# A GRU scan woven into attention on one core: row order of Y, operand tiles, a subtracting scan, staged Newton steps and heads in pairs

## The chip, the cores and the metric

The kernel runs on one core of one Trainium2 chip. The metric is the device time of one execution in microseconds. The engines are TensorE (PE: matmuls; PEld: its weight loads), VectorE (DVE), ScalarE (ACT), GpSimd (POOL) and SyncE (SP), which here only issues DMAs.

## The reference

Four residual layers over x of shape (4, 512, 512); cond has shape (4, 512).

```python
# 1: attention, 16 heads of 32, with adaptive norm
scale, shift = split(cond @ W_emb + b_emb)
xn = rms_norm(x, g_norm) * (1 + scale) + shift
q, k, v = heads(xn @ W_qkv); q, k = rms_norm(q, g_q), rms_norm(k, g_k)
o = softmax(q @ k.T / sqrt(32)) @ v
x = x + o + o @ W_out
# 2: a GRU over the 512 positions, state h of (4, 512), starting from cond
gi = x_t @ W_ih + b_ih;  gh = h @ W_hh + b_hh
r = sigmoid(i_r + h_r);  z = sigmoid(i_z + h_z)
n = tanh(i_n + r * h_n)
h = (1 - z) * n + z * h;  x_t = x_t + h
# 3 and 4: causal convolutions with 4 taps per channel, taps from cond
x = x + conv(x, cond);  x = x + conv(x, cond) + b
```

## The kernel before

**Two kinds of work.** The GRU is a chain of 512 steps that can't be taken in parallel. Attention is cut into 16 blocks of 32 positions; block i must be done before step 32 i. After a setup (weights split into two float16 halves, K and V for all positions) and a ramp that does block 0, one loop over t runs the steps, and the attention of later blocks, and the convolution of earlier ones, are filled in between as tasks.

**One step.** All 512 channels of the state lie as 128 partitions by 16 columns (4 channel groups, 4 batches). PE multiplies the state by the three gates' weights with the state as the stationary operand (L1227, `mm`), into four groups of output rows at once: gates r and z into tile X (128 x 256), gate n into tile Y (128 x 128). The state is carried as three numbers: HS in float32, A its float16 rounding, and the difference. For X 32 matmuls run, 16 with A on the low half of the weights and 16 with the difference and A on the high half; for Y 32 with 16 stationary columns. Both tiles were seeded by ScalarE beforehand with the input's part (L1121 seedX, L1124 seedY) from G, which SyncE loads from a DRAM scratch GD four steps at a time (L1092, L1093).

Each group of 32 rows of Y holds for each of 4 batches 4 slots, which the scan N later runs through: the two parts of the hidden product, the input's part of gate n, and the float16 product again. The four slots of one batch are made by four of the 16 stationary columns.

Then the vector engines follow, in this order of the program: VectorE transposes X in blocks of 32 (TX, L1241) and adds its two parts (S, L1243); ScalarE takes tanh into zt (L1244), seeds X for the next step (L1121) and makes d0 = 0.5 - 0.5 zt, that is 1 - z (L1247); VectorE transposes Y (TY, L1253) and runs the scan N (L1254), which multiplies by r and adds; ScalarE's second tanh gives the first half of D1 (L1255); VectorE gives the second half (L1256) and runs the scan twice, for A (L1264) and HS (L1265), state = d0 * state + D1. Last comes `prep` for the next step: VectorE subtracts A from HS into the operand tile BT (L1130), ScalarE copies A into BT (L1131) and halves HS into HH (L1132), and GpSimd adds HS to x for the convolution (L1269, x2b).

**The queue.** `Queue` places tasks by priorities and planned costs. `head(...)` at the start of a step issues the stages that VectorE, ScalarE and GpSimd owe, within planned budgets; `pe(PE_SLOT)` issues PE's chunks behind Y's matmuls, up to 1600 planned ns a step (2000 in the first 40). A task also takes and returns buffers: PSUM banks `m` (2) and `s` (2), score buffers `P` and so on. `flush` runs the queue to the end of a block that isn't done in time. All five engines run in the order of the program.

For each head, `sch` gives 3 chunks of 4 score matmuls (L439, ps), `smax` the row maximum (L446) and its scaled negative on GpSimd (L447), `sexp` the exponential (L455), `tpch`/`tps` the transposes (L301, ptp) and their copy (L475), and `avch` the product with V (L483, po). Before that comes Q (L369), the squares' sums R with a reciprocal root by three Newton iterations on GpSimd (`rsqrt_ops`, L257 to L276), and after it the output projection WO and the gates' input parts GI (L568).

PSUM has eight banks: X, N, Y (the rest of Y's bank takes `keep_warm`'s idle matmuls), two of m, two of s, one O.

Of the kernel before, what the change touches and what calls it, by code (L numbers as in the profile page):

```python
# [16 lines left out]
P = 128  # L17
# [5 lines left out]
PE_SLOT = 1600  # L23
SC_ = 215
SLOT0, NS0 = 2000, 40
# [10 lines left out]
COLS = {SC_: 192, 680: 256, 137: 64, 150: 128, 330: 128, 140: 256, 111: 256, 123: 256}  # L36
# [126 lines left out]
def body(ctx, tc, x, cond, W_emb, b_emb, g_norm, W_qkv, g_q, g_k, W_out, W_ih, W_hh, b_ih, b_hh, L3_b, out):  # L163
# [9 lines left out]
    NN = pg.tile([P, 16, 4], F32, name="N")  # L173
    Yb = pg.tile([P, 512], F32, name="Y")
    Y, idle = Yb[:, 0:128], Yb[:, 128:512]
# [12 lines left out]
    def rowmask(n, c):  # L188
        m = cst.tile([P, 1], F32, name=n)
        nc.vector.tensor_reduce(m, ident.rearrange("p (q s) -> p q s", q=4)[:, :, c], AX.XY, ALU.add)  # L190
        return m

    mr = mz = rowmask("mr", slice(0, 4))
    mh, mn = rowmask("mh", slice(4, 8)), rowmask("mn", slice(12, 16))

# [33 lines left out]
    BT = [cst.tile([P, 4, 8, 4], F16, name=f"BT{i}") for i in range(2)]  # L229
    for i in range(2):  # L230
        nc.gpsimd.memset(ZT[i], 1.0)
        nc.gpsimd.memset(ZT[i][:, :, :, 0:1], 0.0)
        nc.gpsimd.memset(D0[i], 0.0)
        nc.gpsimd.memset(BT[i], 0.0)
# [7 lines left out]
    def keep_warm(n, to=None):  # L242

        for _ in range(n):
            nc.tensor.matmul(idle if to is None else to, zz[:, 0:128], zz[:, 0:384], start=to is not None, stop=True, skip_group_check=True)
# [73 lines left out]
    q_ = Queue(dict(m=2, s=2, O=1, P=4, PT=4, xb=3, xhl=1, QS=3, q=1, o=1, gi=1, x1=3, L=3))  # L319

    def block_tasks(i):
# [72 lines left out]
        def rs0():  # L394
            v = at("rv", [P, 16])
            rt = at("rt", [P, 4, 32])
            nc.vector.transpose(rt.rearrange("p j r -> p (j r)"), s["pr"][:, 0:128])
            nc.vector.tensor_scalar(v.rearrange("p (j q) -> p j q", j=4), rt[:, :, 0:4], 1.0 / 32, EPS, ALU.mult, ALU.add)
            rq = at("rq", [P, 16])
            s["mx"] = at("mx", [P, 16], bufs=3)  # L400
            s["nb"] = at("nb", [P, 16], bufs=3)
            s["ls"] = at("ls", [P, 16], bufs=3)
            s["rs"] = rq, v
            if not pre_q:
                rsqrt(rq, v, 16, ear, nc.gpsimd)
                rs1()
# [8 lines left out]
        if pre_q:  # L415
            R = Task(f"R{i}")
            R.started, R.done = True, 0
            for tag in ("xb", "QS", "L"):
                q_.free[tag] -= 1
        else:  # L420
            R = add(f"R{i}", deps=[Q], acq=["m", "L"], chunks=[(330, rch)], stages=[[("DVE", 410, rs0), ("Pool", 4800, lambda: None)]], rel=["m", "q"], settle=2)
# [9 lines left out]
        def sch(j, q, u):  # L431
            def f():
                if u == 0:
                    s[("s", j, q)] = pb.tile([P, 512], F32, name="ps", tag="s", bufs=2)
                t = s[("s", j, q)]
                R_ = slice(32 * q, 32 * q + 32)
                x_, k_ = (("qh", KH), ("qh", KL), ("ql", KH))[u]
                for b in range(B):
                    nc.tensor.matmul(t[32 * b:32 * b + 32, :], s[x_][R_, j, 32 * b:32 * b + 32], k_[R_, j, b, :],  # L439
                                     start=(u == 0), stop=(u == 2), skip_group_check=True)  # L440
            return f
# [17 lines left out]
        def tpch(h, ps=False):  # L459
            def piece(j):  # L460
                def f():
                    if j == 0:
                        s[("pt", h)] = pb.tile([P, 512], F32, name="ptp", tag="s" if ps else "m", bufs=2)
                    transpose4(s[("pt", h)], s["PX"][h], (j,))
                return f
            return [(150, piece(j)) for j in range(4)]
# [21 lines left out]
        for j in range(4):  # L488
            for q in range(4):
                h = 4 * j + q  # L490
                STask[h] = add(f"S{i}.{h}", h, deps=[R], acq=["s", "P"], after=last["S"], chunks=[(SC_, sch(j, q, u)) for u in range(3)],
                               stages=[[("DVE", 600, smax(j, q)), ("Pool", 150, lambda: None)], [("ACT", 720, sexp(j, q))]],
                               rel=["s"], settle=int(first))
                last["S"] = [STask[h]]
                TPs[h] = add(f"TP{i}.{h}", h, deps=[STask[h]], after=last["TP"], acq=["m", "PT"], chunks=tpch(h),
                             stages=[[("ACT", 490, tps(h))]], rel=["m", "P"], settle=int(first))
                last["TP"] = [TPs[h]]
                dep = [TPs[h]] + ([prev_av] if prev_av else [])
                AVs[h] = add(f"AV{i}.{h}", h, deps=dep, chunks=[(137, avch(h, kt)) for kt in range(4)],
                             acq=["O"] if h == 0 else [], rel=["PT"])  # L500
                prev_av = AVs[h]
# [100 lines left out]
        def tail(nx, ahead):  # L602
# [42 lines left out]
            def gik(k):  # L645
                for n in "rzn":
                    if k == 0:
                        pg[n] = pm("pgn") if n == "n" else pb.tile([P, 512], F32, name="pgi" + n, tag="s", bufs=2)
                    for m, (xa, wi) in enumerate(((xh, 0), (xl, 0), (xh, 1))):
                        nc.tensor.matmul(pg[n], xa[:, k, :], WR[n][:, wi, k, :], start=(k == 0 and m == 0), stop=(k == 3 and m == 2))  # L650
# [46 lines left out]
    with ExitStack() as pre_ctx:  # L697
# [83 lines left out]
        def x_t(i, tag=None):  # L781
            PY[i] = pb.tile([P, 512], F32, name="py", tag=tag, bufs=2 if tag == "s" else 1) if tag else pm("py")
            transpose4(PY[i], YS[i])
# [137 lines left out]
        def proj(v, kt, b):  # L921
            p = pb.tile([P, 512], F32, name="pkv", tag="s", bufs=2)
            XH, XL = XHL[kt]
            n = 0
            for k in range(4):
                for (xa, wi) in ((XH, 0), (XL, 0), (XH, 1)):
                    nc.tensor.matmul(p, xa[:, k, b, :], WKV[:, wi, k, v, :], start=(n == 0), stop=(n == 11))
                    n += 1
            return p
# [130 lines left out]
    def scan_constants():  # L1060
# [4 lines left out]
        for v, m in ((sel, 1), (selY, 2)):  # L1065
            nc.gpsimd.memset(v, 0.0)
            nc.gpsimd.tensor_scalar(v[:, :, 4 * m:4 * m + 4], ident.rearrange("p (b t) -> p t b", b=4)[:, 0:2, :], 1.0, 1.0,
                                    ALU.mult, ALU.mult)

    sel, selY = lt("sel", [P, 2, 8]), lt("selY", [P, 2, 12])  # L1070
# [3 lines left out]
    with tc.manual_schedule(engines={ENG.PE, ENG.DVE, ENG.Activation, ENG.Pool, ENG.SP}):  # L1074
        ahead = [t for t in need[1] if t.name in ("S1.0", "S1.1", "S1.2")]
# [3 lines left out]
        q_.flush(need[0] + ahead, 1700, lambda used: keep_warm(max(0, int((1050 - used) / 160))), {8: scan_constants})  # L1079
# [9 lines left out]
    def load_g(c):  # L1089
        g, i, t0_ = G[c % 2], c // 8, 4 * (c % 8)  # L1090
        for qq in range(4):
            nc.sync.dma_start(g[32 * qq + 4:32 * qq + 8, :, 0:2, :], GD[i][qq, :, t0_:t0_ + 4, 0:2, :])  # L1092
            nc.sync.dma_start(g[32 * qq + 8:32 * qq + 12, :, 2, :], GD[i][qq, :, t0_:t0_ + 4, 2, :])  # L1093
# [3 lines left out]

    def dup(v):
        return v.rearrange("p (k b) -> p k b", k=4).unsqueeze(2).to_broadcast([P, 4, 2, 4])


    def seed_first(t, y):
# [12 lines left out]
        for qq in range(4 * y):  # L1115
            r = 32 * qq
            nc.tensor.matmul(Y[r:r + 12, :], selY[:, t], gs0["n"][:, qq, :], start=False, stop=True,
# [8 lines left out]
    def prep(A, HS, t):  # L1126

        Bt = BT[t % 2]
        HH = wk.tile([P, 16], F32, name="HH", tag="HH")
        nc.vector.tensor_tensor(Bt[:, :, 0:4:2, :], dup(HS[:, :, 1]), dup(A[:, :, 1]), ALU.subtract)  # L1130
        nc.scalar.activation(Bt[:, :, 1:8:2, :], A[:, :, 1].rearrange("p (k b) -> p k b", k=4).unsqueeze(2).to_broadcast([P, 4, 4, 4]), AF.Copy)  # L1131
        nc.scalar.activation(HH, HS[:, :, 1], AF.Copy, scale=0.5)  # L1132
        return Bt, HH

# [65 lines left out]
    with tc.manual_schedule(engines={ENG.PE, ENG.DVE, ENG.Activation, ENG.Pool, ENG.SP}):  # L1200
        seed_first(0, 0)
        Bt, HH = prep(A, HS, 0)
        due = None
        for t in range(T):
# [27 lines left out]
            for k in range(4):  # L1232
                mm(X, Bt[:, k, 0:2, :].rearrange("p s b -> p (s b)"), 8, Whi, k, slice(0, 2))
            if t == 0:
                seed_first(0, 1)
            for k in range(4):
                mm(Y, Bt[:, k, 4:8].rearrange("p s b -> p (s b)"), 16, Wlo, k, slice(2, 3))
            for k in range(4):
                mm(Y, Bt[:, k, 0:4].rearrange("p s b -> p (s b)"), 16, Whi, k, slice(2, 3))
# [13 lines left out]
            nc.vector.transpose(TY.rearrange("p h j b k -> p j h k b"), Y.rearrange("p (j h k b) -> p j h k b", j=4, h=2, k=4))  # L1253
            nc.vector.tensor_tensor_scan(f(NN), f(zt[:, 0]), TY[:, 0].rearrange("p j b k -> p (j b k)"), 0.0, ALU.mult, ALU.add)  # L1254
            nc.scalar.activation(D1[:, :, 0], NN[:, :, 3], AF.Tanh, scale=0.5 * IWS)  # L1255
            nc.vector.scalar_tensor_tensor(D1[:, :, 1], zt[:, 1, :, 2], 1.0, HH, ALU.add, ALU.mult)  # L1256
# [6 lines left out]
            keep_warm(-(-(WARM - q_.cols) // 384), pm("warm")[:, 0:384] if q_.free["m"] else None)  # L1263
            nc.vector.tensor_tensor_scan(f(An), f(d0), f(D1), 0.0, ALU.mult, ALU.add)  # L1264
            nc.vector.tensor_tensor_scan(f(HSn), f(d0), f(D1), 0.0, ALU.mult, ALU.add)  # L1265
            A, HS = An, HSn
            if t + 1 < T:
                Bt, HH = prep(A, HS, t + 1)
# [30 lines left out]
```

## Time and profile before

| | |
|---|---|
| Timed runs | 1883.12, 1876.41, 1889.18 us; median 1883.12 us |
| Profiled execution | 1878.9 us, span 1876.8 us, 114,013 instructions |
| PE busy | 1655.3 us (88%) |
| DVE busy | 1344.8 us (72%) |
| ACT busy | 1220.1 us (65%) |
| POOL busy | 468.6 us (25%) |
| Mean granted clock of PE | 0.982 |

The scan's N runs 512 times, from 242.9 to 1856.7 us; what lies before is setup and ramp, what lies behind is the last convolution. Busy shares are means over all of this. A matmul's end is modelled, and matmuls overlap, so a busy PE need not be the bound; which wait ends last in a step decides that. A group's line on the page gives the program line, the engine, output and inputs, sizes, count, busy time, the mean of one in ns, and the idle time before it with what ended it.

### The profile page before, as it was taken

How to read it: one execution, taken by the hardware profiler on the slowest of the kernel's cores; microseconds unless marked ns; L12 is line 12 of the kernel's file. 1: busy time of each engine (PE TensorE's matmuls, PEld its weight loads, DVE VectorE, ACT ScalarE, POOL GpSimd, SP SyncE). 2: the span in 40 equal slices, each digit the busy share in tenths (PEclk: the TensorE clock that was granted, in tenths of full speed). 3: DMA queues.
4: the chain of work that ended last, by engine and by line, in shares of the span. 5: the costliest groups of instructions: out<-in, count | busy, mean ns of one | idle time of the engine just before them, and what ended most of it. 6: DMA issues, size and time to landing. Idle time of an engine off the chain costs nothing.

```text
span 1876.8 us, 114013 instructions
## 1 busy us (share of the span) xinstructions
PE 1655.3 (88%) x48969; PEld 1173.1 (63%) x48969; DVE 1344.8 (72%) x4948; ACT 1220.1 (65%) x4685; POOL 468.6 (25%) x1496
## 2 busy tenths in 40 slices
PE   5788889999999999999999999999999998987553
PEld 2443557667676767676767666676667676765442
DVE  4784467786778777877777777878777877776664
ACT  4542466776767776767676767676676767665543
POOL 1366001222213131222222131313131222121112
PEclk9998899999999999999999999999999999999998
DMA  5652020101010102010101010010101010101000
GB/s 184 226 191 91 25 68 18 50 18 34 18 35 13 39 16 60 13 39 13 40 12 34 19 49 25 19 35 13 39 13 40 13 34 12 35 13 34 11 17 10
DMA packets 68921, 78.11 MB, mean 42 GB/s; under 512 B 6560, under 2 KB 54720, under 8 KB 67776
## 3 DMA queue, kind: packets, MB, share of 16 engines
q1 hardware_dynamic: 68416, 70.82, 12.5%
q8 instruction: 385, 6.31, 1.4%
q14 instruction: 120, 0.98, 0.2%
HBM read 44.58 MB, written 26.21 MB: 38 GB/s over the span
## 4 chain that ended last, share of the span: by engine, by line
PE 47%; DVE 24%; ACT 10%; DMA 8%; issue 6%; SPq 3%; POOL 2%; DVEq 0%; ACTq 0%; POOLq 0%
PE X L1227 21%; PE ps L439 6%; DVE TX L1241 5%; PE Y L1227 5%; PE pgi L568 5%; DMA G<-GD 5%; DVE TY L1253 4%; PE ptp L301 4%; DVE N L1254 4%; ACT D L1255 3%; DVE A L1264 2%; PE po L483 2%; ACT X L1121 2%; SPq L1093 2%; ACT Y L1124 1%
## 5 line engine op out<-in xcount | busy, mean ns | idle before, releaser
L1227 PEld LDWEIGHTS <-BT 128*8 128x8 f16 (+1 forms) x24576 | 450.2, 88 | 82.5 <-issue 19.1
L1227 PE MATMUL X<-Wlo,A 128*4 128x256 f16 x8192 | 313.1, 272 | 126.4 <-DVE A L1264 88.9
L1269 POOL TENSOR_TENSOR x2b<-x,HS 128x16 f32<-128x16 f32 x512 | 126.8, 248 | 1130.7 <-DVE HS L1265 1129.4
L1244 ACT ACTIVATE ZT<-S 128x32 f32<-128x32 f32 x512 | 134.9, 264 | 415.8 <-DVE S L1243 415.3
L1241 DVE STREAM_TRANSPOSE TX<-X 128x256 f32<-128x256 f32 x512 | 229.2, 448 | 210.0 <-PE X L1227 208.9
L1227 PE MATMUL X<-Whi,BT 128*8 128x256 f16 x8192 | 316.0, 273 | 2.7 <-issue 2.4
L1227 PEld LDWEIGHTS <-A 128*4 128x4 f16 x8192 | 151.4, 82 | 219.1 <-DVE A L1264 192.4
L1253 DVE STREAM_TRANSPOSE TY<-Y 128x128 f32<-128x128 f32 x512 | 205.2, 401 | 11.1 <-PE Y L1227 5.0
L1227 PE MATMUL Y<-Whi,BT 128*16 128x128 f16 x8192 | 209.2, 219 | 4.3 <-issue 4.0
L1227 PE MATMUL Y<-Wlo,BT 128*16 128x128 f16 x8192 | 207.9, 219 | 4.2 <-issue 3.7
L1121 ACT ACTIVATE X<-G 128x256 f32<-128x256 f32 x510 | 202.4, 397 | 1.1 <-DMA G<-GD 0.9
L455 ACT ACTIVATE PX<-ps,nb,rqs 128x512 f32<-128x512 f32 x256 | 195.1, 762 | 8.7 <-POOL nb L447 4.8
L1254 DVE TENSOR_TENSOR_SCAN N<-ZT,TY 128x64 f32<-128x64 f32 x512 | 153.3, 299 | 54.9 <-ACT ZT L1244 1.9
L446 DVE TENSOR_REDUCE mx<-ps 128x1 f32<-128x512 f32 x256 | 174.8, 683 | 16.0 <-PE ps L439 15.9
L1264 DVE TENSOR_TENSOR_SCAN A<-D,D 128x32 f16<-128x32 f32 x512 | 115.2, 225 | 94.2 <-ACT D L1255 91.5
L301 PE MATMUL ptp<-ident,PX 128*128 128x128 f32 x1024 | 173.3, 290 | 1.0 <-ACT gs L576 0.6
L1131 ACT ACTIVATE BT<-A 128x64 f16<-128x64 f16 x512 | 131.2, 256 | 52.8 <-DVE A L1264 4.6
L301 PEld LDWEIGHTS ptp<-ident,PX 128*128 128x128 f32 x1024 | 111.4, 143 | 81.7 <-issue 43.1
L475 ACT ACTIVATE PT<-ptp 128x512 f32<-128x512 f32 x248 | 143.3, 582 | 15.7 <-PE ptp L301 15.7
L1124 ACT ACTIVATE Y<-G 128x128 f32<-128x128 f32 x510 | 141.6, 278 | 1.0 <-DMA G<-GD 0.5
L483 PEld LDWEIGHTS po<-V,PT 128*32 128x32 f32 x8192 | 99.1, 112 | 62.5 <-issue 53.8
L483 PE MATMUL po<-V,PT 128*32 128x32 f32 x8192 | 131.1, 200 | 7.3 <-issue 6.5
(266 smaller groups left out, 2818.7 us busy)
## 6 DMA issues: line engine op xcount, KB each, us to landing
GD<-gs SPq DMA_DIRECT2D x45, 256.0 KB
G<-GD SPq DMA_DIRECT2D x512, 16.0 KB
G<-GD SPq DMA_DIRECT2D x512, 8.0 KB
xp<-in_x_dram SPq DMA_DIRECT2D x16, 256.0 KB
xb<-in_x_dram SPq DMA_DIRECT2D x16, 256.0 KB
xhl<-XD SPq DMA_DIRECT2D x32, 128.0 KB
out_dram<-ob SPq DMA_DIRECT2D x16, 256.0 KB
wst<-in_L_cond_W_qkv_dram SPq DMA_DIRECT2D x6, 512.0 KB
```

Of the source, the lines that this page charges most:

```text
L301: nc.tensor.transpose(dst[:, 128 * j:128 * j + 128], src[:, 128 * j:128 * j + 128], ident)
L446: nc.vector.tensor_reduce(s["mx"][:, h:h + 1], s[("s", j, q)], AX.X, ALU.max)
L455: nc.scalar.activation(pe_, s[("s", j, q)], AF.Exp, bias=s["nb"][:, h:h + 1], scale=s["rqs"][:, h:h + 1], accum_out=s["ls"][:, h:h + 1])
L475: nc.scalar.activation(pt_, s[("pt", h)], AF.Copy)
L483: nc.tensor.matmul(s["po"][32 * b:32 * b + 32, 32 * h:32 * h + 32], s["PT"][h][:, kt, 32 * b:32 * b + 32], V[:, 4 * b + kt, 32 * h:32 * h ...
L1121: nc.scalar.activation(X.rearrange("p (g c) -> p g c", g=2), G[(t // 4) % 2][:, t % 4, 0:2, :], AF.Copy)
L1124: nc.scalar.activation(Y, G[(t // 4) % 2][:, t % 4, 2, :], AF.Copy)
L1227: nc.tensor.matmul(dst[32 * qq:32 * qq + M, :], lhs, W[:, k, cols].rearrange("p g (j q s) -> p q g j s", j=4, q=4)[:, qq], start=False, st ...
L1241: nc.vector.transpose(TX.rearrange("p a r -> p (a r)"), X)
L1253: nc.vector.transpose(TY.rearrange("p h j b k -> p j h k b"), Y.rearrange("p (j h k b) -> p j h k b", j=4, h=2, k=4))
L1254: nc.vector.tensor_tensor_scan(f(NN), f(zt[:, 0]), TY[:, 0].rearrange("p j b k -> p (j b k)"), 0.0, ALU.mult, ALU.add)
L1264: nc.vector.tensor_tensor_scan(f(An), f(d0), f(D1), 0.0, ALU.mult, ALU.add)
```

## The change

- **Rows of Y.** The 16 stationary columns go by batch and then slot, where they went by slot and then batch. TY's output is then contiguous in runs of 16. Slots are ordered A, difference, difference, A, and both weight halves use the same columns. The seeds' rows in G, the masks for the biases and selY move with them.
- **Operand tiles.** BX for X (two slots) and BY for Y (four) take the place of BT. VectorE subtracts for BX, GpSimd for BY; ScalarE copies A into both.
- **The state's scan subtracts.** D1's first half is tanh of the negative argument, its second (d0 - 1) * HS, and the two scans compute d0 * state - D1. HH goes.
- **Newton steps.** R's reciprocal root is issued in three further stages, one iteration each, in place of one.
- **Heads in pairs.** A task SP issues the score matmuls of two heads by turns, with a planned cost of 225 for 8 matmuls. N moves into columns 128 to 191 of Y's bank, and s gets a third bank. `keep_warm` writes only to a free m bank.
- **Budgets.** PE_SLOT 1550 for 1600, the first 40 steps 1900 for 2000.

```diff
-PE_SLOT = 1600
-SC_ = 215
-SLOT0, NS0 = 2000, 40
+PE_SLOT = 1550
+SC_ = 225
+SLOT0, NS0 = 1900, 40
...
-    NN = pg.tile([P, 16, 4], F32, name="N")
-    Y, idle = Yb[:, 0:128], Yb[:, 128:512]
+    Y, NN = Yb[:, 0:128], Yb[:, 128:192].rearrange("p (a k) -> p a k", k=4)
...
-q_ = Queue(dict(m=2, s=2, ...
+q_ = Queue(dict(m=2, s=3, ...
...
             if not pre_q:
-                rsqrt(rq, v, 16, ear, nc.gpsimd)
-                rs1()
+                s["nw"] = rsqrt_ops(rq, v, 16, ear, nc.gpsimd)
+                next(s["nw"])
+                next(s["nw"])
+
+        def rsp(last):
+            def f():
+                for _ in range(3 if not last else 9):
+                    next(s["nw"], None)
+                if last:
+                    rs1()
+            return f
...
-  stages=[[("DVE", 410, rs0), ("Pool", 4800, lambda: None)]], rel=["m", "q"], settle=2)
+  stages=[[("DVE", 410, rs0)]] + [[("Pool", 700, rsp(n == 2))] for n in range(3)], rel=["m", "q"], settle=1)
...
                 for b in range(B):
-                    nc.tensor.matmul(t[32 * b:32 * b + 32, :], s[x_][R_, j, ...], k_[R_, j, b, :], ...)
+                    for r in (q, q + 1):
+                        R_ = slice(32 * r, 32 * r + 32)
+                        nc.tensor.matmul(s[("s", j, r)][32 * b:32 * b + 32, :], s[x_][R_, j, ...], k_[R_, j, b, :], ...)
...
+                if q % 2 == 0:
+                    SP = add(f"SP{i}.{h}", h, deps=[R], acq=["s", "s", "P", "P"], after=last["S"],
+                             chunks=[(SC_, sch(j, q, u)) for u in range(3)], settle=1)
...
-            nc.sync.dma_start(g[32 * qq + 8:32 * qq + 12, :, 2, :], GD[i][qq, :, t0_:t0_ + 4, 2, :])
+            nc.sync.dma_start(g[32 * qq + 2:32 * qq + 18:4, :, 2, :], GD[i][qq, :, t0_:t0_ + 4, 2, :])
...
     def prep(A, HS, t):
-        Bt = BT[t % 2]
-        HH = wk.tile([P, 16], F32, name="HH", tag="HH")
-        nc.vector.tensor_tensor(Bt[:, :, 0:4:2, :], dup(HS[:, :, 1]), dup(A[:, :, 1]), ALU.subtract)
-        nc.scalar.activation(Bt[:, :, 1:8:2, :], A[:, :, 1]...to_broadcast([P, 4, 4, 4]), AF.Copy)
-        nc.scalar.activation(HH, HS[:, :, 1], AF.Copy, scale=0.5)
-        return Bt, HH
+        Bx, By = BX[t % 2], BY[t % 2].rearrange("p k b s -> p (k b) s")
+        h4, a4 = (v[:, :, 1].rearrange("p (k b) -> p k b", k=4) for v in (HS, A))
+        two = lambda v: v[:, :, 1].unsqueeze(2).to_broadcast([P, 16, 2])
+        nc.vector.tensor_tensor(Bx[:, :, 0], h4, a4, ALU.subtract)
+        nc.gpsimd.tensor_tensor(By[:, :, 1:3], two(HS), two(A), ALU.subtract)
+        nc.scalar.activation(Bx[:, :, 1], a4, AF.Copy)
+        nc.scalar.activation(By[:, :, 0:4:3], two(A), AF.Copy)
+        return Bx, BY[t % 2]
...
-            nc.vector.transpose(TY.rearrange("p h j b k -> p j h k b"), Y.rearrange("p (j h k b) -> p j h k b", j=4, h=2, k=4))
+            nc.vector.transpose(TY.rearrange("p h j b k -> p j h (b k)"), Y.rearrange("p (j h r) -> p j h r", j=4, h=2))
             nc.vector.tensor_tensor_scan(f(NN), f(zt[:, 0]), TY[:, 0]..., 0.0, ALU.mult, ALU.add)
-            nc.scalar.activation(D1[:, :, 0], NN[:, :, 3], AF.Tanh, scale=0.5 * IWS)
-            nc.vector.scalar_tensor_tensor(D1[:, :, 1], zt[:, 1, :, 2], 1.0, HH, ALU.add, ALU.mult)
+            nc.scalar.activation(D1[:, :, 0], NN[:, :, 3], AF.Tanh, scale=-0.5 * IWS)
+            nc.vector.scalar_tensor_tensor(D1[:, :, 1], d0[:, :, 1], 1.0, HS[:, :, 1], ALU.subtract, ALU.mult)
...
-            keep_warm(-(-(WARM - q_.cols) // 384), pm("warm")[:, 0:384] if q_.free["m"] else None)
-            nc.vector.tensor_tensor_scan(f(An), f(d0), f(D1), 0.0, ALU.mult, ALU.add)
-            nc.vector.tensor_tensor_scan(f(HSn), f(d0), f(D1), 0.0, ALU.mult, ALU.add)
+            if q_.free["m"]:
+                keep_warm(-(-(WARM - q_.cols) // 384), pm("warm")[:, 0:384])
+            nc.vector.tensor_tensor_scan(f(An), f(d0), f(D1), 0.0, ALU.mult, ALU.subtract)
+            nc.vector.tensor_tensor_scan(f(HSn), f(d0), f(D1), 0.0, ALU.mult, ALU.subtract)
```

## The prediction

> **What bounds the kernel now.** Part 4 of the profile page comes first, and it misleads here: it puts a fifth of the chain on the scan's matmuls and a sixth on attention work (ps, pgi, ptp, po), as if TensorE were the bound.
>
> ```profile
> PE X L1227 21%; PE ps L439 6%; DVE TX L1241 5%; PE Y L1227 5%; PE pgi L568 5%; DMA G<-GD 5%; DVE TY L1253 4%; PE ptp L301 4%; DVE N L1254 4%; ACT D L1255 3%; DVE A L1264 2%; PE po L483 2%; ACT X L1121 2%; SPq L1093 2%; ACT Y L1124 1%
> ```
>
> Ends of matmuls are modelled, so that chain crosses to TensorE wherever a filler's modelled end passes the start of X. The view of the waits is firmer: nearly every step has ScalarE waiting for S, VectorE for X, and TensorE's weight load for A.
>
> ```profile
> ACT ZT L1244 <- DVE S L1243: 415.3, 470, 2.3
> DVE TX L1241 <- PE X L1227: 208.9, 420, 1.8
> PEld L1227 <- DVE A L1264: 192.4, 343, 1.6
> ```
>
> So I read one plain step in the timeline, engine by engine: VectorE, ScalarE, and the weight load that opens the next step (start, length, engine, line). This step's X began at 1003.03.
>
> ```profile
> 1004.12 0.45 DVE L1241 STREAM_TRANSPOSE TX<-X 128x256 f32<-128x256 f32 x1 [0.81 <-PE X L1227]
> 1004.61 0.19 DVE L1243 TENSOR_TENSOR S<-TX 128x32 f32<-128x32 f32 x1
> 1004.72 0.40 DVE L1253 STREAM_TRANSPOSE TY<-Y 128x128 f32<-128x128 f32 x1
> 1005.22 0.30 DVE L1254 TENSOR_TENSOR_SCAN N<-ZT,TY 128x64 f32<-128x64 f32 x1
> 1005.43 0.16 DVE L1256 SCALAR_TENSOR_TENSOR D<-ZT,HH 128x16 f32<-128x16 f32 x1
> 1005.77 0.22 DVE L1264 TENSOR_TENSOR_SCAN A<-D,D 128x32 f16<-128x32 f32 x1 [0.18 <-ACT D L1255]
> 1005.91 0.20 DVE L1265 TENSOR_TENSOR_SCAN HS<-D,D 128x32 f32<-128x32 f32 x1
> ```
> ```profile
> 1004.83 0.27 ACT L1244 ACTIVATE ZT<-S 128x32 f32<-128x32 f32 x1 [1.46 <-DVE S L1243]
> 1004.97 0.40 ACT L1121 ACTIVATE X<-G 128x256 f32<-128x256 f32 x1
> 1005.31 0.21 ACT L1247 ACTIVATE D<-ZT 128x16 f32<-128x16 f32 x1
> 1005.55 0.18 ACT L1255 ACTIVATE D<-N 128x16 f32<-128x16 f32 x1
> ```
> ```profile
> 1006.09 0.32 PEld L1227 LDWEIGHTS <-A 128*4 128x4 f16 x16 [0.23 <-DVE A L1264]
> ```
>
> The step is 3.06 us, and it is a chain: X's matmuls 1.09, TX to S 0.49, S to TY 0.11, TY to N 0.50, N to the second tanh 0.33, tanh to A 0.22, A to the next X 0.32. A's line says what it waited for: 0.18 us for ScalarE's tanh. Counted over the trace, the next X starts 0.055 us after A's end in 456 of 511 steps, fillers or not. The tile view has N from 242.9 to 1856.7, a mean step of (1856.7 - 242.9)/511 = 3.16 us; the last two blocks, with little filler, go at 3.02. So 0.14 x 511 = 72 us lies above the bare chain: about 25 of it VectorE or TensorE being late with TX, 15 TY starting late, 25 X starting late after A, of which 17 in the first 64 steps (the longest one 5.6 us at step 61, the flush of block 2).
>
> **The change, part by part.**
>
> **TY in row order.** TY now writes with a 16-byte stride and takes 401 ns. The contiguous transpose of the same size, rt, takes 308; the new one writes runs of 16 floats. So its price lies between 308 and 401; I take 308.
>
> ```profile
> L1253 DVE STREAM_TRANSPOSE TY<-Y 128x128 f32<-128x128 f32 x512 | 205.2, 401 | 11.1 <-PE Y L1227 5.0 <-ACT D L1247 1.6 <-ACT ZT L1244 1.4
> ...
> L397 DVE STREAM_TRANSPOSE rt<-pr 128x128 f32<-128x128 f32 x16 | 4.9, 308 | 0.0
> ```
>
> N would start at 1005.13 for 1005.22 (it also needs ZT, done at 1005.10), and tanh and all after it 0.09 earlier. That would be 0.09 x 511 = 46 us, if tanh stayed the last thing A waits for.
>
> **The state's scan subtracts.** It doesn't stay so. L1256 now reads zt and HH, both long done, and runs in the shadow of tanh. The new line reads d0, which ScalarE makes at L1247, and that instruction stands behind the seed of X (0.40 us), where the diff leaves it. d0 ends at 1005.31 + 0.21 = 1005.52. VectorE starts 0.03 after ScalarE's end (A after tanh), so D1 starts at 1005.55 instead of 1005.43 and ends at 1005.71. A depends on D1 on its own engine and also on ScalarE; N is such a scan with two waits, and it starts 0.10 after TY's end (1005.12 to 1005.22). So A starts at 1005.81 instead of 1005.77. Behind D1 in VectorE's queue stand A and HS, behind A the next X. The wait for tanh is gone and one for D1 takes its place: **0.04 us later per step, whatever TY gains**. Worked through for every step with its own times it is 0.039 in the median and 0.046 in the mean, since in a quarter of the steps d0 lies later against A: 512 x 0.046 = +23.6 us. In some hundred steps X starts late for TensorE's sake anyway and swallows its share, about 4: **+19 us**. HH (203 ns) leaves ScalarE at the step's start, where ScalarE waits for S 415 us over the run: nothing.
>
> **Operand tiles.** ScalarE writes 16 and 32 elements instead of 64 and HH: two instructions either way (203 for 16, 264 for 32, against 256 and 203), and X's second half needs them 0.43 after X's start, when they are done by 0.2. VectorE's subtract falls from 32 to 16 elements (192 to some 175 ns, D1's row being 163); this counts only where VectorE's other work delays TX, some 90 steps: -1.4 us. GpSimd gets a new subtract of 32 elements: between x2b's 248 (16) and 456 (128), near the lower; I take 0.28. It starts with HS's end, as x2b does, 0.14 after X's start, and ends at 0.42; Y's matmuls begin 0.87 after X. The 0.45 us between are its cover; without it Y, and then TY, come later one for one. X2b queues behind it, and nobody in the step waits for that. As for the port between the two engines: BT beside x2b takes 192 ns, the same as S alone, but 0.35 at 1006.14 beside GpSimd's 0.46 us tap.
>
> The Trainium skill's "SBUF — State Buffer", section "Who interferes with whom", speaks against this part: a VectorE instruction with two SBUF inputs contends with a GpSimd instruction that reads SBUF. By the rule the new subtract could stretch VectorE's own each time; by the row of BT beside x2b it doesn't. With 0.35 for every step X's second half would start 0.1 later, +50 us; I follow the row and put nothing in the sum.
>
> **Newton in stages.** 14 GpSimd instructions of 0.22 at a spacing of 0.30 held x2b back by 2.3 us (1003 to 1005.32). Split, a step gets 4 (1.2 us) or 6 (1.8 us), so the new subtract is not behind them. Cost on the path nothing; the scores of a block may start two steps later, and one m bank is held three steps more. Steady blocks finish their last gate at step 310 when 318 is due, so there is room.
>
> **Heads in pairs, N in Y's bank.** N moves so that scores have three banks; all users of that bank are ordered already (Y, TY, N, tanh, seed of Y), so no wait. A block has 48 chunks at 0.216; in pairs 24 of about 0.23. That two heads do run side by side is in the trace, where the last chunk of one head meets the first of the next:
>
> ```profile
> 199.32 0.40 PE L439 MATMUL ps<-KH,ql 32*32 32x512 f16 x4
> 199.33 0.39 PE L439 MATMUL ps<-KH,qh 32*32 32x512 f16 x4
> 199.56 0.38 PE L439 MATMUL ps<-KL,qh 32*32 32x512 f16 x4
> ```
>
> The second starts 0.01 after the first, not 0.22, and both together take 0.24. So 10.4 - 5.5 = 4.9 us of TensorE per block, 73 over 15. It is hidden: the fillers end before A does. What counts is the first 64 steps with their 17 us of late X: budgets 1900 for 2000 and fewer chunks, -3.4; the flush of 5.6 us misses its date by one step and I give it even odds of going, -2.5 (0 to -5.6). The ramp before the scan (176 to 221 us) waits for VectorE and ScalarE by turns: -1.5 (-4 to +3). The changed masks, the seeds' rows 4 apart and keep_warm's condition keep their counts of instructions and of DMAs (512 of 8 KB), which land steps ahead: 0.
>
> **Sum:** 19.3 - 3.4 - 2.5 - 1.4 - 1.5 = +10.5 us on the profiled execution's 1878.9 (span 1876.8 and 2.1 around it): 1889.4. The three timed runs have a median of 1883.1, 4 above that execution, so I say **1890**. Its own range: the chain from 15 (more swallowed) to 24, the rest from -14 to 0, and a few us for another order of the queue: 1876 to 1910.
>
> **Rivals.**
>
> **D1's wait costs nothing.** If tanh stays last, A comes 0.09 earlier: 46 us, of which a quarter of the steps lose some part, because fillers issue to within 0.2 us of X: -35, with the small terms -9: 1835. For it: A idles for tanh 503 times. Against: d0's place behind the seed is plain in the timeline.
>
> **TensorE is the bound after all**, as part 4 says. Then half of ps's 6% (53 us) goes: 1878.9 - 53 + 19 = 1845. Against: the constant 0.055.
>
> **The GpSimd subtract sets the pace (slower).** If VectorE's subtract is stretched to 0.35 beside it, X's second half comes 0.1 later in each step: 1890 + 51 = 1941. It decides from 0.1 us of stretch on, since the operand is ready about 0.1 before its matmul. The BT row speaks against it.
>
> **Pairs run one after the other (slower).** Then a chunk takes 0.43 for 0.225 planned; three make 0.62, of which 0.3 is idle time: 120 x 0.3 = 36: 1926. Against: the 0.01 us above.
>
> **Chances.** Forecast 0.80, free wait 0.09, TensorE 0.04, GpSimd 0.04, pairs 0.03. 1% is about what a measurement of this kernel can tell from no change, 19 us. Faster by more: 0.09 + 0.04 = 0.13. Slower by more: 0.07 and the forecast's upper part, 0.14, together 0.21. Within: 0.66. The range goes down to 1845 to take in the TensorE case and up to 1912; left out are 0.09 below and 0.07 above and a little of the tails.
>
> **What would show it.** Right: D1 starts about 0.12 later after X than now and 0.03 after d0's end; A no longer waits for tanh but 0.10 after D1; bare steps of the last blocks at 3.06 instead of 3.02; TY near 310 ns; ps chunks of 8 matmuls 0.23 apart; TensorE's busy share down by 3 to 4 points. Wrong: bare steps at 2.93, A still on tanh, or TX later than 1.10 after X.

## The result, and the profile after

The changed kernel takes 1914.24 us, the median of four runs (1907.47 to 1915.57); the kernel before, four runs on the same chip, 1883.55 us (1876.41 to 1889.18). The ratio is **1.0164**, 95% interval 1.0135 to 1.0192: slower by 1.6%. The forecast was 1890 with a range up to 1912. The profiled execution after took 1907.47 us (span 1905.7) against 1878.9 (span 1876.8): +28.6.

Part 4 of the page after, the chain that ended last, by engines and by lines:

```profile
DVE 34%; PE 31%; ACT 20%; issue 7%; DMA 3%; POOL 2%; DVEq 1%; SPq 1%; ACTq 0%; POOLq 0%
PE X L1238 22%; DVE TX L1252 10%; ACT X L1130 7%; DVE A L1276 6%; ACT ZT L1255 5%; DVE S L1254 4%; DVE D L1267 4%; ACT D L1258 3%; PE ps L450 2%; DVE mx L457 2%; DVE x L1172 2%; PE Y L1238 2%; ACT PX L466 1%; PE ptp L301 1%; DVEq L1276 1%
```

It has moved from TensorE to VectorE: TX has 10% for 5%, A 6% for 2%, and D1 (L1267), which had no place, 4%. The page's first part has PE's busy time down from 88% to 82% of the span, more than the 3 to 4 points that were forecast.

```profile
PE 1571.8 (82%) x48986; PEld 1150.6 (60%) x48986; DVE 1332.9 (70%) x4948; ACT 1247.8 (65%) x4685; POOL 563.1 (30%) x2006
```

So 83 us of TensorE's work are gone and the kernel is longer. The view of the waits after (what waited, on what; us in total, times, longest):

```profile
PEld L1238 <- DVE A L1276: 312.7, 403, 3.5
PE X L1238 <- DVE A L1276: 228.0, 372, 3.3
...
DVE A L1276 <- ACT D L1266: 12.9, 46, 0.4
```

In the kernel before, the last of these lines was:

```profile
DVE A L1264 <- ACT D L1255: 91.5, 503, 0.7
```

TensorE's weight load waits for A for 313 us where it waited 192, and A waits for the second tanh in 46 steps where it did in 503. The timeline of a step without attention work (step 490; X began at 1818.08) shows what A waits for instead, on VectorE and on ScalarE, and then the next step's weight load:

```profile
1819.18 0.45 DVE L1252 STREAM_TRANSPOSE TX<-X 128x256 f32<-128x256 f32 x1 [0.24 <-PE X L1238]
1819.66 0.19 DVE L1254 TENSOR_TENSOR S<-TX 128x32 f32<-128x32 f32 x1
1819.77 0.31 DVE L1264 STREAM_TRANSPOSE TY<-Y 128x128 f32<-128x128 f32 x1
1820.18 0.30 DVE L1265 TENSOR_TENSOR_SCAN Y<-ZT,TY 128x64 f32<-128x64 f32 x1
1820.59 0.18 DVE L1267 SCALAR_TENSOR_TENSOR D<-D,HS 128x16 f32<-128x16 f32 x1
1820.90 0.22 DVE L1276 TENSOR_TENSOR_SCAN A<-D,D 128x32 f16<-128x32 f32 x1
```
```profile
1820.02 0.39 ACT L1130 ACTIVATE X<-G 128x256 f32<-128x256 f32 x1
1820.35 0.21 ACT L1258 ACTIVATE D<-ZT 128x16 f32<-128x16 f32 x1
1820.57 0.19 ACT L1266 ACTIVATE D<-Y 128x16 f32<-128x16 f32 x1
```
```profile
1821.17 0.32 PEld L1238 LDWEIGHTS <-A 128*4 128x4 f16 x16 [1.58 <-DVE A L1276]
```

Three places are to be read here. D1 (L1267) starts at 1820.59, 0.03 after d0 (L1258) ended at 1820.56: as forecast. D1 takes 0.18 and A starts at 1820.90, **0.13 after D1's end** and not 0.10. And tanh (L1266) starts 0.09 after N's end (1820.48), where it was 0.03 before; that one is hidden here, since tanh ends 0.14 before A starts. The step lasts 3.10 us; the kernel before has 3.02 there.

Two more views: the groups of TY, and the score matmuls in PE's timeline after.

```profile
L1264 DVE STREAM_TRANSPOSE TY<-Y 128x128 f32<-128x128 f32 x512 | 158.1, 309 | 8.6 <-PE Y L1238 4.2
```
```profile
999.74 0.41 PE L450 MATMUL ps<-KH,qh 32*32 32x512 f16 x8
999.96 0.40 PE L450 MATMUL ps<-KL,qh 32*32 32x512 f16 x8
1000.18 0.40 PE L450 MATMUL ps<-KH,ql 32*32 32x512 f16 x8
```

TY takes 309 ns instead of 401, and a chunk of eight matmuls comes every 0.22 us: both parts do what was forecast of them.

### The profile page after: what moved, and what is told of

Same layout as the page of the kernel before. It is cut to its first block, busy times and chain, and to the rows that moved or that the text cites. A ratio compares the mean times of both kernels' runs of the same rounds, so it can differ in the third digit from the quotient of the medians.

```text
span 1905.7 us, 115633 instructions
## 1 busy us (share of the span) xinstructions
PE 1571.8 (82%) x48986; PEld 1150.6 (60%) x48986; DVE 1332.9 (70%) x4948; ACT 1247.8 (65%) x4685; POOL 563.1 (30%) x2006
## 4 chain that ended last, share of the span: by engine, by line
DVE 34%; PE 31%; ACT 20%; issue 7%; DMA 3%; POOL 2%; DVEq 1%; SPq 1%; ACTq 0%; POOLq 0%
PE X L1238 22%; DVE TX L1252 10%; ACT X L1130 7%; DVE A L1276 6%; ACT ZT L1255 5%; DVE S L1254 4%; DVE D L1267 4%; ACT D L1258 3%; PE ps L450 2%; DVE mx L457 2%; DVE x L1172 2%; PE Y L1238 2%; ACT PX L466 1%; PE ptp L301 1%; DVEq L1276 1%
## 5 line engine op out<-in xcount | busy, mean ns | idle before, releaser
L1141 POOL TENSOR_TENSOR BY<-HS,A 128x32 f16<-128x32 f32 x512 | 127.3, 249 | 1135.3 <-DVE HS L1277 1114.2
L1238 PE MATMUL X<-Whi,BX 128*8 128x256 f16 x8192 | 316.8, 273 | 1.9 <-issue 1.2
L1238 PEld LDWEIGHTS <-BY 128*16 128x16 f16 x16384 | 276.4, 90 | 25.2 <-issue 11.8
L1238 PE MATMUL Y<-Whi,BY 128*16 128x128 f16 x8192 | 208.6, 219 | 5.1 <-issue 5.0
L1238 PEld LDWEIGHTS <-BX 128*8 128x8 f16 x8192 | 178.0, 86 | 53.0 <-issue 4.8
L1238 PE MATMUL Y<-Wlo,BY 128*16 128x128 f16 x8192 | 207.5, 219 | 3.0 <-issue 1.5
L1265 DVE TENSOR_TENSOR_SCAN Y<-ZT,TY 128x64 f32<-128x64 f32 x512 | 153.5, 300 | 56.4 <-ACT X L1130 2.3
L301 PE MATMUL ptp<-ident,PX 128*128 128x128 f32 x1024 | 164.2, 286 | 4.6 <-ACT PX L466 1.4
L1264 DVE STREAM_TRANSPOSE TY<-Y 128x128 f32<-128x128 f32 x512 | 158.1, 309 | 8.6 <-PE Y L1238 4.2
L1142 ACT ACTIVATE BX<-A 128x16 f16<-128x16 f16 x512 | 110.9, 217 | 47.3 <-DVE A L1276 2.5
```

The source lines that it names most:

```text
L301: nc.tensor.transpose(dst[:, 128 * j:128 * j + 128], src[:, 128 * j:128 * j + 128], ident)
L1238: nc.tensor.matmul(dst[32 * qq:32 * qq + M, :], lhs, W[:, k, cols].rearrange("p g (j q s) -> p q g j s", j=4, q=4)[:, qq], start=False, st ...
L1264: nc.vector.transpose(TY.rearrange("p h j b k -> p j h (b k)"), Y.rearrange("p (j h r) -> p j h r", j=4, h=2))
```

## The experiments

Below, the **floor** is the step that 10% of the 511 steps stay under, measured from X's first matmul to the next X's: the bare chain. What the steps take beyond 511 floors is called the **rest** (mostly attention's delays), and the **ramp** is the time up to the first X. All three are read from one profiled execution of each kernel; starts and lengths given in ns or to 0.001 us are medians over the steps. The diffs are shortened, and parts of them are put in words. Before: floor 3.018 us, rest 72 us, ramp 240.2 us. After: 3.100, 66 and 233.0. So the chain gave 511 x 0.082 = 42 us, and rest and ramp gave 13 back.

**Theory 1:** the loss lies in the chain from N to A, in the number of engines that tanh and A wait for and in D1's dependence on d0. **Theory 2:** it lies on the side of attention and of the operand tiles.

Two pieces are first put alone into the kernel before.

**e3, the subtracting scan alone**

```diff
-D1[..., 0] = tanh(0.5 * N);   D1[..., 1] = (zt + 1) * HH
+D1[..., 0] = tanh(-0.5 * N);  D1[..., 1] = (d0 - 1) * HS
-scan(A, HS): d0 * state + D1
+scan(A, HS): d0 * state - D1
```

> The kernel before with only the subtracting scan (D1 from d0 and HS, no HH). Theory 1: D1 starts at d0's end, 2.515 us after X's start, takes 0.176, and A follows 0.10 later, at 2.79 instead of 2.74: 0.05 x 511 = 26 us more than before, about 1909 us. Theory 2: no change, 1883 us.

Measured: 1905.78 us, ratio 1.0128 [1.0092, 1.0165]; floor 3.076. This one edit costs 58 ns a step, more than the 39 that the prediction gave it. D1 starts 0.03 after d0 as forecast, but takes 176 ns with d0 and HS as operands, 163 with zt and HH. A starts 0.103 after D1's end, as the prediction took from N. So 13 of the missing 19 ns are D1's length. Step 490 shows it, VectorE first and then ScalarE:

```profile
1818.78 0.18 DVE L1254 SCALAR_TENSOR_TENSOR D<-D,HS 128x16 f32<-128x16 f32 x1
1819.06 0.23 DVE L1262 TENSOR_TENSOR_SCAN A<-D,D 128x32 f16<-128x32 f32 x1
```
```profile
1818.54 0.21 ACT L1245 ACTIVATE D<-ZT 128x16 f32<-128x16 f32 x1
1818.79 0.18 ACT L1253 ACTIVATE D<-N 128x16 f32<-128x16 f32 x1
```

**e4, pairs, N in Y's bank, the third score bank and the budgets alone**

```diff
-NN = pg.tile([P, 16, 4], F32, name="N")
+NN = Yb[:, 128:192]
-Queue(dict(m=2, s=2, ...
+Queue(dict(m=2, s=3, ...
+SP: score matmuls of two heads by turns; SC_ 225, PE_SLOT 1550, SLOT0 1900
```

> The kernel before with only the attention side of the change: heads in pairs, N in Y's bank, a third score bank, the new budgets; Newton, operand tiles, row order and D1 as before. Theory 1: tanh reads N from a tile that TensorE also writes and gets a second wait, so it starts 0.06 later, which is now on the path: +30 us; the ramp gains 7 and the later X of the first blocks about 10: about 1896 us. If the bank costs nothing on the path, only the gains are left: about 1866 us. Theory 2 (the attention side is the loss): 1905 us or more.

Measured: 1890.24 us, ratio 1.0042 [1.0023, 1.0061]; floor 3.082, rest 58, ramp 233.7. The attention side gains: 14 us of rest (the flush at step 61 is gone) and 6.6 of ramp. The floor loses 64 ns, 33 us. The timelines of step 490, VectorE and then ScalarE, show where:

```profile
1804.11 0.30 DVE L1258 TENSOR_TENSOR_SCAN Y<-ZT,TY 128x64 f32<-128x64 f32 x1
1804.31 0.16 DVE L1260 SCALAR_TENSOR_TENSOR D<-ZT,HH 128x16 f32<-128x16 f32 x1
1804.72 0.23 DVE L1269 TENSOR_TENSOR_SCAN A<-D,D 128x32 f16<-128x32 f32 x1 [0.24 <-ACT D L1259]
```
```profile
1804.50 0.19 ACT L1259 ACTIVATE D<-Y 128x16 f32<-128x16 f32 x1
```

N ends at 1804.41 and tanh starts at 1804.50. The profile names N's tile "Y" now, and that is the point: tanh reads a tile that TensorE writes, so it waits for TensorE's semaphore as well as VectorE's, though Y's matmuls are long done when N ends. The trace's record of semaphores bears this out: in the kernel before, tanh itself waits for VectorE, and in e4 a separate semaphore instruction of 17 ns ahead of it does, while tanh itself waits for TensorE. The second wait costs 60 ns (94 instead of 33, medians over the steps), and here it is on the chain, because tanh is the last thing A waits for.

The next two change one thing in the kernel after.

**e1, d0 ahead of the seed of X on ScalarE**

```diff
+nc.scalar.activation(d0[:, :, 1], zt[:, 1, :, 2], AF.Copy, scale=-0.5, bias=0.5)
 seedX(t + 1)
-nc.scalar.activation(d0[:, :, 1], zt[:, 1, :, 2], AF.Copy, scale=-0.5, bias=0.5)
```

> The changed kernel with one swap on ScalarE: d0 is made before the seed of X, not behind it. Theory 1 (the loss sits between N and A): D1 no longer waits for d0 and ends under tanh, at about 2.49 us after X's start instead of 2.69; A then follows tanh's end (2.68), about 0.09 behind it because A waits for three engines, so at 2.77 instead of 2.82: 0.05 x 511 = 26 us less, about 1888 us. Theory 2 (the loss is on the attention side: pairs, queue, banks): D1 moves but the time stays within 5 us of 1914.

Measured: 1908.66 us, ratio to before 1.0133 [1.0102, 1.0165]; floor 3.073. The waits show the chain change hands:

```profile
DVE A L1276 <- ACT D L1266: 142.0, 505, 3.5
```

A waits for tanh in 505 steps again, so D1's wait is gone, and still the floor is 55 ns over that of before. d0 must await zt's end, so it begins 0.29 after zt's start where the seed had begun 0.14 after it. In the last two blocks the seed then ends at 2.60 after X's start and tanh begins at 2.54, where it began at 2.50 in the kernel after, and A starts 87 ns behind tanh instead of 32. Taking D1's wait away brought the chain onto the seed ahead of tanh and onto the waits of tanh and A.

**e2, GpSimd copies the difference out of BX**

```diff
-nc.gpsimd.tensor_tensor(By[:, :, 1:3], two(HS), two(A), ALU.subtract)
+nc.gpsimd.tensor_scalar(BY[..., 1:3], Bx[:, :, 0] twice, 1.0, 1.0, ALU.mult, ALU.mult)
```

> The changed kernel, but GpSimd makes its half of BY by copying the difference from BX, so it no longer reads A. Theory 1: A's write then has no wait for GpSimd; its waits go from three to two and it follows D1's end by 0.10 us instead of 0.13: 0.028 x 511 = 14 us less, about 1900 us. If GpSimd's work or the port were what costs, a later start of this copy (it now waits for VectorE's subtract) would make it no faster or slower: 1914 or more.

Measured: 1927.81 us, ratio 1.0236 [1.0206, 1.0266]; floor 3.123. A's start falls from 0.132 to 0.103 after D1's end, now that GpSimd no longer reads A. But GpSimd now reads BX, as the view of the waits shows:

```profile
POOL BY L1141 <- DVE BX L1140: 1149.9, 490, 19.2
```

So BX's next writer, VectorE's subtract, must wait for GpSimd as well as for VectorE. Its distance from HS's end is 0.03 in the kernel after (the first two lines) and 0.10 in e2 (the last two):

```profile
1817.94 0.20 DVE L1277 TENSOR_TENSOR_SCAN HS<-D,D 128x32 f32<-128x32 f32 x1
1818.17 0.17 DVE L1140 TENSOR_TENSOR BX<-HS,A 128x16 f16<-128x16 f32 x1
```
```profile
1837.13 0.20 DVE L1277 TENSOR_TENSOR_SCAN HS<-D,D 128x32 f32<-128x32 f32 x1
1837.43 0.18 DVE L1140 TENSOR_TENSOR BX<-HS,A 128x16 f16<-128x16 f32 x1
```

The subtract starts 0.165 after X's start instead of 0.095, X's second half at 0.49 instead of 0.435, TX at 1.147 instead of 1.097. 29 ns were won at A and 50 lost at BX. The wait wasn't removed but moved to another instruction of the chain. That this edit comes out slower was not foreseen.

From here on parts of the change are undone one after another. **e5, N in SBUF; e6, D1 from zt and HH again; e7, both; e8, e7 with GpSimd taking the float16 state from BY, ScalarE's copy, instead of from A:**

```diff
 # e5, e7, e8
-NN = Yb[:, 128:192]
+NN = cst.tile([P, 16, 4], F32, name="N")
 # e6, e7, e8
+nc.scalar.activation(HH, HS[:, :, 1], AF.Copy, scale=0.5)
-D1[..., 1] = (d0 - 1) * HS;  scans subtract
+D1[..., 1] = (zt + 1) * HH;  scans add
 # e8
-nc.gpsimd.tensor_tensor(By[:, :, 1:3], two(HS), two(A), ALU.subtract)
 nc.scalar.activation(By[:, :, 0:4:3], two(A), AF.Copy)
+nc.gpsimd.tensor_tensor(By[:, :, 1:3], two(HS), By[:, :, 0:1] twice, ALU.subtract)
```

> The changed kernel with N in SBUF instead of Y's bank. Theory 1: tanh loses its wait for TensorE and ends some 40 ns earlier, but A waits for D1, which waits for d0, and comes at 2.82 us after X's start as before: no gain, 1914 us within 6. If the time were lost in Y's bank itself, the 30 us that the pairs alone seem to cost there (0.06 us a step) would come back: about 1884.

> The changed kernel with D1 from zt and HH again (scans add). Theory 1: D1 is out of the way; tanh ends at 2.68 after X's start, late by its wait for TensorE, and A follows 0.09 behind it because it still waits for three engines: 2.77 instead of 2.82, 0.05 x 511 = 27 us less, about 1887 us. If the subtracting scan were the whole loss: all of 80 ns a step, about 1873 us or less.

> As e6, with N in SBUF. Theory 1: tanh has one wait and starts 0.06 earlier, and takes some 25 ns more from SBUF; A at about 2.73 after X's start: 20 us less than e6, about 1867 us. If two waits on one instruction cost nothing: as e6.

> As e7, and GpSimd takes its float16 state from BY, where ScalarE has put it, instead of from A, so A's write needn't wait for GpSimd. Theory 1: A follows tanh by 0.03 instead of 0.09, at about 2.68 after X's start; bare steps 2.96 us against 3.02 in the kernel before: about 1839 us, faster than both kernels. The subtract on GpSimd starts some 0.25 us later and still ends before Y's matmuls at 0.87; if it doesn't, TY is late and the time is above 1870.

Measured, all four against 1873.11 us of before on their chip:

| | us | ratio, interval | floor |
|---|---|---|---|
| e5 | 1910.85 | 1.0202 [1.0172, 1.0232] | 3.102 |
| e6 | 1884.83 | 1.0058 [1.0036, 1.0080] | 3.046 |
| e7 | 1878.68 | 1.0019 [0.9997, 1.0040] | 3.025 |
| e8 | 1855.19 | 0.9896 [0.9862, 0.9931] | 2.970 |

e5 leaves the floor where it was: while D1 is last, tanh's extra wait costs nothing. e6 takes 54 ns off, and with it tanh is last again, so that e7 against e6 shows tanh's wait in its own price: 60 ns less wait, 43 more because tanh takes 229 ns from SBUF and 186 from PSUM, and N 7 less. e8 against e7 shows the third wait of A. VectorE and ScalarE in e7:

```profile
1794.44 0.23 DVE L1279 TENSOR_TENSOR_SCAN A<-D,D 128x32 f16<-128x32 f32 x1 [0.28 <-ACT D L1269]
```
```profile
1794.12 0.23 ACT L1269 ACTIVATE D<-N 128x16 f32<-128x16 f32 x1
```

and in e8:

```profile
1776.43 0.23 DVE L1279 TENSOR_TENSOR_SCAN A<-D,D 128x32 f16<-128x32 f32 x1 [0.23 <-ACT D L1269]
```
```profile
1776.17 0.23 ACT L1269 ACTIVATE D<-N 128x16 f32<-128x16 f32 x1
```

Tanh ends at 1794.35 and A starts at 1794.44; in e8, 1776.40 and 1776.43. The arithmetic is the same and so is the order of the engines. In e7 A must wait for GpSimd to have read its tile; in e8 GpSimd reads BY, and A waits for VectorE and ScalarE alone: 55 ns of floor, 23 us of time. **e8 beats both kernels**, but by less than was expected: its floor is the expected one within 0.01, while its rest is 81 us (77 in e7, 72 in the kernel before), so that part of the chain's gain was lost to attention's delays.

Last, the same edits without the pairs. **e9 is the kernel before with row order, operand tiles and Newton stages; e10 is e9 with GpSimd reading BY; e11 is e10 with pairs and their budgets, but two score banks, N keeping its own; e12 is e10 with Newton in one stage.**

```diff
 # e9, e10, e11, e12: rows of Y, BX and BY; D1 from zt and HH, scans add, N in a bank of its own
 # e10, e11, e12
-nc.gpsimd.tensor_tensor(By[:, :, 1:3], two(HS), two(A), ALU.subtract)
+nc.gpsimd.tensor_tensor(By[:, :, 1:3], two(HS), By[:, :, 0:1] twice, ALU.subtract)
 # e11
+SP for two heads, acq s, s, P, P; SC_ 225, PE_SLOT 1550, SLOT0 1900; s=2
 # e12
-stages=[[("DVE", 410, rs0)]] + [[("Pool", 700, rsp(n == 2))] for n in range(3)]
+stages=[[("DVE", 410, rs0), ("Pool", 4800, lambda: None)]]
```

> The kernel before with the order of the rows of Y by batch and slot (TY as one contiguous transpose), the operand tiles BX and BY (GpSimd's subtract reads HS and A) and the Newton steps in three stages; D1 from zt and HH with scans that add, N in a bank of its own, heads singly and the budgets as before. Theory 1 (the loss sits in the chain from N to A, in what each instruction there waits for): N comes at 2.10 us as in the changed kernel, tanh waits for one engine and runs 2.435 to 2.62, A waits for three engines (GpSimd reads A) and starts 0.087 after tanh, at 2.71 instead of 2.742; floor step 2.985 to 2.99 against 3.017, 15 to 17 us of 511 steps, so about 0.991 of the time before. Theory 2 (what was lost lies on the attention side, in the tiles or the Newton stages as much as in the chain): not faster than before, 0.998 or more.

> The kernel of the run above, but GpSimd takes the float16 state for its subtract from BY (ScalarE's copy) instead of from A, so that no GpSimd instruction reads A. Theory 1: A waits for two engines again and starts 0.032 after tanh, at 2.65; floor step 2.93; a further 25 to 28 us off, about 0.976 of the time before, less what late attention work takes back (in the kernel with N in SBUF and this edit it took some 10 us), so 0.975 to 0.982. Theory 2: no more than 0.3% from the run above.

> The kernel of the run above with the heads' score matmuls in pairs and the budgets of the changed kernel, with two score banks only, since N keeps a bank of its own. What the pairs are worth: the ramp before the scan 6 to 7 us shorter as in the run of the pairs alone, 0.003 below the run above, if two banks are enough. If a pair that needs both banks at once holds up the queue, X starts late after A by more than the 25 ns a step of before, and the time is above the run above: by 5 to 25 us.

> The kernel of the second run of this call (rows, tiles, GpSimd reads BY) with the Newton steps in one stage of 14 GpSimd instructions, as before the change. The prediction held that the stages cost nothing and serve to keep GpSimd's subtract on time: if the subtract stands behind 14 instructions of some 0.3 us in one or two steps of each of 14 blocks, the matmuls of Y wait for it by 1 to 3 us there: 20 to 40 us over the second run. If the instructions fall where the subtract is not due, or DVE's order keeps them apart: within 5 us of it.

Measured against 1877.16 us of before; rest and ramp from the profiled executions, in us:

| | us | ratio, interval | floor | rest | ramp |
|---|---|---|---|---|---|
| e8 (above) | 1855.19 | 0.9896 [0.9862, 0.9931] | 2.970 | 81 | 237.9 |
| e9 | 1896.94 | 1.0107 [1.0073, 1.0140] | 2.989 | 100 | 244.7 |
| e10 | 1880.78 | 1.0015 [0.9994, 1.0037] | 2.935 | 109 | 252.5 |
| e11 | 1943.91 | 1.0348 [1.0314, 1.0382] | 2.933 | 170 | 243.4 |
| e12 | 1879.76 | 1.0022 [0.9998, 1.0047] | 2.936 | 119 | 252.4 |

The floors are those that theory 1 gave, within 6 ns, and the times are not: it had e9 at 0.991 and e10 at 0.976. The chain's gain goes back in full to the rest and the ramp. In e9 and e10 the step at 61, where block 2 is flushed, takes 13.7 and 13.3 us (8.6 before), and steps 189 and 349 take 10.0 to 10.1 each (3.3 and 3.0 before). So theory 2 holds here: the queue without pairs doesn't finish these blocks in time. It isn't the short chain alone that does it, since e12 below has the same floor without these flushes; Newton's stages have a part in it. Set e8 beside e10: e8's floor is 35 ns longer (18 us) and yet its ratio is 0.012 lower (22 us). Pairs with a third bank, and their budgets, are then worth some 40 us (by the table 28 of rest, 19 of them in the steps 61, 189 and 349, and 15 of ramp), where on the chain of before, with Newton in one stage (e4), they were worth 21. The 15 are uncertain, because the ramp differs between executions of one kernel (last section).

e11 shows that the bank is part of it. A pair takes both banks at once, and with two of them 43 steps take over 4 us (7 before), the longest 12.2. Its time is 63 us over e10, where 5 to 25 were expected if the banks hold up the queue. The ramp, 9 us shorter than e10's in these executions, is 3 us longer than that of before.

e12 is a miss in the other direction. GpSimd's subtract does stand behind Newton there; the waits of e12 show Y late for it:

```profile
DVE TY L1261 <- PE Y L1235: 27.9, 25, 1.8
PEld L1235 <- POOL BY L1138: 27.5, 17, 2.1
```

In e10 the same two lines are:

```profile
DVE TY L1262 <- PE Y L1236: 6.1, 16, 1.2
PEld L1236 <- POOL BY L1139: 0.4, 2, 0.2
```

But the time is that of e10: in e12 the steps 61, 189 and 349 take 8.6, 3.1 and 2.9 us. One stage costs some 22 us at Y, three stages cost two flushes and a longer one in this kernel, some 19 us. The prediction's "Cost on the path nothing" holds for the stages in the kernel after as far as the flushes go, and not here. In the kernel after, with pairs, there are no such flushes at 189 and 349; what the stages are worth there wasn't tried.

## Why the prediction was wrong, step by step

**The mechanism was right.** D1 becomes last, starts 0.12 later and 0.03 behind d0, and TY's gain of 0.09 is lost: e3 has the loss without TY's gain at all, e5 shows that nothing on tanh's side counts while D1 is last.

**The step that failed is the size of the chain's term**, "0.039 in the median and 0.046 in the mean", from "A starts at 1005.81". By the trace's segments, summed over the steps, TY's start to A's start costs +46.1 us where +23.6 stood. The missing 22.5 are D1's 176 ns for 163 (13 ns, seen alone in e3) and A's start 0.132 after D1 for 0.103 (29 ns, gone in e2; e8 takes the same wait away where tanh is last). Together 42 ns x 511 = 21 us. The row taken for A's start, N behind TY, has two waits. A has three: VectorE, ScalarE, and GpSimd, which must have read A's old tile. The prediction followed what the new subtract writes forward, and found 0.45 us of cover before Y; it is 0.42 in the trace, and Y is not late. It didn't follow it backward, to the next writer of what it reads.

**"All users of that bank are ordered already (...), so no wait"** was wrong in the same way: the order made the wait useless, not absent. It costs tanh 60 ns, hidden in the kernel after, and 31 us on the path in e4.

**The small terms.** X late after A gave -10.1 where -4, -3.4 and -2.5 stood, right in the sum; but the flush at step 61 stayed (7.7 us), so the odds on it were lost and made up elsewhere, by luck as far as the runs tell. TX and what delays it: +2.9 instead of -1.4. TY after S: -2.6 for nothing. The ramp: -7.2, outside its bounds of -4 to +3. It goes with the granted clock (last section), which no step of the prediction looked at.

The sum: 46.1 + 2.9 - 2.6 - 10.1 - 7.2 = +29.1 against +28.9 of span. The forecast of the profiled execution missed by 18 us; the other 6 are the distance from that execution, the shortest of the four, to their median. The prediction had read a distance of 4 for the kernel before and did not add it.

**The rivals.** "D1's wait costs nothing" did not come. TensorE as the bound did not come in the kernel after; in e9 to e12 attention's queue took back what the chain gained, which doesn't show TensorE itself as the bound. The count against this rival was too high: the next X starts 0.055 to 0.056 after A's end in 406 steps and within 0.11 in 456, so the argument stands with a smaller number. The GpSimd subtract takes 248 ns (0.28 estimated) and Y is not late for it. The rule of the Trainium skill's "SBUF — State Buffer", section "Who interferes with whom", holds in part. BX's subtract starts 0.11 ahead of GpSimd's, overlaps it for 0.06, and keeps the 175 ns that it has in e10, where the two don't overlap. But in e9 VectorE's first tap of the convolution takes 409 ns in the 89 of 192 cases where it starts 0.02 ahead of GpSimd's subtract; in e10, where that subtract starts 0.2 later, the taps beside it take 345 to 351. In a step without attention work TX begins 1.097 after X either way, so it costs nothing there. The rival's other figure, an operand ready "about 0.1" before its matmul, was too large: in e2 the subtract comes 0.07 later and X's second half 0.053 later. The pairs run side by side.

## What to carry to other kernels

Before a step on a chain of small instructions is changed, count for each the engines it waits for, including those that must have finished with the tile it overwrites or shares: a further one cost 0.03 to 0.06 us here, up to a third of the instruction itself, even when its signal had long come, wherever the signal that comes last was not the one that the instruction itself waits for. Let an engine off the chain read a copy that another engine off the chain made, as in e8, and keep a tile of the chain out of a bank that TensorE writes. A chain and the work filled into it are tuned to each other: in e10 a floor shorter by 83 ns, 42 us in all, brought nothing, and the same edits with pairs and a third bank (e8) brought 1%.

## What the runs showed of the hardware

**Waits can have a price when they are long satisfied.** VectorE's scan starts 32 ns after ScalarE's end if it waits for ScalarE and its own engine, 87 with GpSimd as a third. Behind its own engine's last instruction it is 103 ns with two, 132 with three. ScalarE's tanh starts 33 ns after VectorE's end, 94 with TensorE as a second wait.

The traces' semaphore records say more than the count. One wait stands on the instruction itself, and the others in a semaphore instruction ahead of it. In all 510 steps from the third on, A with two waits itself waits for ScalarE, and the instruction ahead for VectorE; with three, A itself waits for GpSimd, and the one ahead for both others. When the last signal is the one on the instruction itself, the start comes 32 to 34 ns after it, with one wait (D1, the subtract, tanh) or with two (A in the kernel before and in e8). When the last signal is waited for ahead, the start comes 87 to 132 ns after it. So A's second wait costs nothing behind tanh, and in e3 A follows D1, though tanh ends 0.02 after D1 in the median step.

**The ramp's length goes with the clock granted in it.** The windows of 190 to 205 us, after and in e10 (length, then busy us and instructions of PE, PEld, DVE, ACT, POOL, then the granted clock, DMA share and GB/s):

```profile
190.00:205.00 15.00, 12.80 (x387) 7.16 (x370) 8.88 (x20) 7.28 (x17) 0.00 (x0) 1.00 0.11 40
```
```profile
190.00:205.00 15.00, 14.41 (x245) 8.41 (x240) 5.16 (x13) 6.32 (x14) 0.00 (x0) 0.50 0.17 68
```

At 0.50 TensorE gets through 245 matmuls instead of 387 while looking busier. The kernel before, whose heads go singly as in e10, has 384 there at 1.00, so it isn't the pairs that make this difference. From 175 to 232 us the mean clock is 1.00 in the kernel after, in e1, e2 and e4 to e7 (first X at 233.0 to 234.9), 0.91 in e8 (237.9), 0.82 before and in e3 (240.2 and 242.2), 0.76 in e9 (244.7), 0.57 in e10 and e12 (252.5 and 252.4); e11, which also lacks a bank, has 0.88 (243.4). What lowers it there was not tried, and one execution of each kernel doesn't tie it to the edit: 23 executions of the kernel before have mean clocks over the whole span of 0.971 to 0.984, and their times, 1868 to 1887 us, fall as the clock rises, by some 14 us per 0.01. The profiled executions of e10 and e12 are the longest of twelve each. "TensorE: Matmul & The Clock Gate" of the Trainium skill, Part 1, says that half rate is the default state and that activity releases it; that the ramp's 0.50 is this state is not shown by any run here.

**Sources.** The same tanh of 16 elements takes 186 ns from PSUM and 229 from SBUF on ScalarE.
